# Attention output projection with the four heads packed in 128 rows and channels on partitions

## The chip, the cores and the metric

The kernel runs on one core of a Trainium2 chip. A core has a matrix engine (TensorE, PE in the profile), a vector engine (VectorE, DVE), an activation engine (ScalarE, ACT), a general engine (GpSimd, POOL) and a queue that issues transfers (SyncE, SP). Each takes its own instructions in the order in which the program issues them, and waits at an instruction until what it needs is there. The metric is the time of one execution on the device in microseconds.

## The reference, cut to what matters

Layer 0 is attention with 4 heads of 32 channels over 4 images of 64 x 64 pixels and 128 channels, then a projection, a residual and a norm over the channels. Layer 1 takes its result and adds a 3 x 3 convolution, a spectral term and a mamba block (a selective scan along the pixels). All is float32.

```python
Q, K, V = (split_heads(x_flat @ W + b) for W, b in ((Wq, bq), (Wk, bk), (Wv, bv)))
attn = softmax(einsum('bhnd,bhmd->bhnm', Q, K) * scale)
out = einsum('bhnm,bhmd->bhnd', attn, V)           # then heads side by side: 128 channels
y = out @ Wo + bo + x_flat
y = (y - mean(y)) / sqrt(var(y) + 1e-5) * gamma + beta      # over the 128 channels
# layer 1, per image:
result = conv3x3(y) + irfft2(spec_w @ rfft2(y)) + mamba(y)
# mamba: in_proj, causal conv of 4 taps, silu, dt/B/C, then per pixel
h = exp(dt * A) * h + dt * B * x;  out = sum_n h * C + D * x;  gate with silu(z);  out_proj
```

## The kernel before

**Tiling.** An image's 4096 pixels are 8 chunks of 512, so there are 32 chunks `c`. The heads are taken in two pairs (`PAIRS = 2`), so there are 64 halves `H`: chunk `H // 2`, pair `H % 2`. For each half the keys run in 32 tiles of 128, and one turn of the main loop is one such tile. A chunk is therefore 64 turns, called steps here.

**A loop turn** issues, in this order: the scores of a key tile with their maximum taken off (`scores_for_exp`, six matmuls L478, then the exponential L486 on ACT); the scores for the maximum of the next half, some steps ahead (`scores_for_max`, four matmuls L434, then the maximum L441 on DVE); at an even step one scan of mamba for an earlier chunk (`scan_state`: scan L793 on DVE, then `state` L796, the multiply `hs` L797 and the sum `acc` L812 on GpSimd); at an odd step the next decay (L780 on ACT), the next input term (`db` L785 on GpSimd) and now and then a load of `bc`; then one turn of the planner; then the product of exponentials and values (`times_values`, four matmuls `po` L498). A record in the profile can be half of a float32 matmul, which is why L498 shows four for two calls.

**The planner** orders everything else. A job is a coroutine that yields what it needs next: "P" a slot on TensorE, "D" one on DVE, "A" one on ACT, "B" one of two PSUM banks, "" just the next step. While attention runs an odd step offers two each of P, D and A, an even step only one A. A job that yields "A" and then "PB" thus issues its ACT work in one odd step and its matmuls in the next odd step. The jobs that matter here are `normalise` (divide a pair's output by its softmax sums), `output_projection` (project, add the residual, statistics of the norm, normalise), `mamba_input`, `scan_input` (the convolution steps L673 and L678), `scan_dt` (its last part is three multiplies on GpSimd, L738 to L740), `gate` and `scan_output`.

**Around the projection.** At the end of a half ACT and DVE copy `po` out of PSUM into `oz[k]` (L507, L508), one tile for each pair. In it a head's 32 output rows start at row 0 or 64, with the softmax sum in the row behind them; the other rows are zeros, written once at the start. `normalise` sends the sums to DRAM (`zd`), reads them back spread over the partitions (`zc`), takes the reciprocal, writes it (`rd`), reads it back broadcast over 64 rows for each head (`rz`, L528), and GpSimd multiplies `oz[k]` by it (L531). `output_projection` adds the bias to the residual `xr` on ACT (L546) and then issues, for each of four 128-pixel tiles, one matmul for each pair against a `Wo` padded with zero rows (L554) and one with the identity that adds the residual (L555). The result `py` has pixels on partitions, and DVE takes the statistics from it (L562 to L568) and writes the normalised `xh` (L585).

```python
yield "A"
nc.scalar.activation(xr, xr, AF.Identity, bias=bo)
bank = yield "PB"
```

Of the kernel before, what the change touches and what calls it, by code (L numbers as in the profile page):

```python
# [9 lines left out]
F32 = mybir.dt.float32  # L10
F32R = mybir.dt.float32r
AF = mybir.ActivationFunctionType
ALU = mybir.AluOpType
# [4 lines left out]
P = 128  # L18
W = 64
HEADS = 4  # L20
HD = P // HEADS
PAIRS = HEADS // 2
HS = P // 2
L = 512
RPC = L // W
TPC = L // P
# [129 lines left out]
def attention_then_conv_mamba(  # L156
# [17 lines left out]
    nc = tc.nc  # L174
    ctx.enter_context(tc.manual_schedule())
    B, C, N = x.shape
    NCH = N // L
# [5 lines left out]
    const = ctx.enter_context(tc.tile_pool(name="const", bufs=1))  # L183
    att = ctx.enter_context(tc.tile_pool(name="att", bufs=2))
# [10 lines left out]
    for h in range(HEADS):  # L195
        k, j = divmod(h, 2)
        nc.scalar.dma_start(wk_t[:, h, :], wk[k, :, j * HS : j * HS + HD])
    wat = const.tile([P, 1 + PAIRS, P], F32, name="wat_vo")
    nc.scalar.dma_start(wat[:, 0, :], wvo[0])
    for h in range(HEADS):  # L200
        k, j = divmod(h, 2)
# [3 lines left out]
        )  # L205
    Wk = wk_t.rearrange("c h d -> c (h d)")
    Wv = wat[:, 0, :]
    Wo = [wat[:, 1 + k, :] for k in range(PAIRS)]

    wq_t = const.tile([P, PAIRS, 2, 2, HD], F32, name="wq_t")  # L210
    bq = const.tile([P, PAIRS], F32, name="bq")
# [13 lines left out]
    nc.scalar.dma_start(cst, consts[:, :K_SEL])  # L225
    sel_f = loc.tile([P, P], F32, tag="sg0", name="sel_f", bufs=1)
    nc.scalar.dma_start(sel_f, consts[:, K_SEL:])
    bvk = const.tile([P, PAIRS], F32, name="bvk")
    nc.vector.memset(wat[:, 1:, :], 0.0)
    nc.vector.memset(bvk, 0.0)  # L230
    for h in range(HEADS):
        row = h % 2 * HS
        hs = slice(h * HD, (h + 1) * HD)
        nc.scalar.dma_start(wat[row : row + HD, 1 + h // 2, :], wvo[1, hs, :])
        nc.scalar.dma_start(
            bvk[row : row + HD, h // 2 : h // 2 + 1], bv[0:1, hs].rearrange("o c -> c o")
        )
    vec = const.tile([P, NCOL], F32, name="vec")
    nc.scalar.dma_start(vec, vecs)
    cw = const.tile([P, 9, P], F32, name="cw")  # L240
# [19 lines left out]
    sel = const.tile([P, P], F32R, name="sel")  # L260
    ones = const.tile([P, 1], F32, name="ones")
    nc.vector.memset(ones, 1.0)
    minus_one = const.tile([P, 1], F32, name="minus_one")
    nc.vector.memset(minus_one, -1.0)
    g = const.tile([P, 3, P], F32, name="g")
# [10 lines left out]
    def constants_of_the_rest():  # L276


        yield ""
        half = loc.tile([P, 2, 2 * P], F32, tag="sg1", name="half", bufs=1)  # L280
        nc.vector.tensor_scalar(half, spw, 0.5, None, ALU.mult)
        rr, ir = half[:, 0, :P], half[:, 0, P:]
        ri, ii = half[:, 1, :P], half[:, 1, P:]
        yield ""
        g_id = loc.tile([P, P], F32, tag="ob", name="g_id", bufs=1)
        nc.gpsimd.tensor_tensor(g_id, rr, ii, ALU.add)
        nc.gpsimd.tensor_tensor(cw[:, 4, :], cw[:, 4, :], g_id, ALU.add)
        nc.gpsimd.tensor_tensor(g_flip, rr, ii, ALU.subtract)
        nc.gpsimd.tensor_tensor(g_hil, ri, ir, ALU.subtract)
        nc.gpsimd.tensor_tensor(g_fliphil, ri, ir, ALU.add)  # L290
        yield ""
        nc.vector.tensor_scalar(sbias, cst[:, K_G : K_G + W], col("spec_bi"), None, ALU.mult)
        nc.vector.tensor_tensor(sbias[:, 0:1], sbias[:, 0:1], col("spec_br"), ALU.add)

        nc.scalar.activation(negA, vec[:, COL["A_log"] : COL["A_log"] + NH * NS], AF.Exp)
        yield ""
        nc.vector.tensor_scalar(negA, negA, -1.0, None, ALU.mult)


        bank = yield "PB"  # L300
        pb = bank_tile(bank, [P, 1], "pb")
        for k in range(PAIRS):
            nc.tensor.matmul(pb, Wo[k], bvk[:, k : k + 1], start=k == 0, stop=k == PAIRS - 1)
        yield "D"
        plan.release(bank, 2)
        nc.vector.tensor_tensor(bo, pb, col("bo"), ALU.add)
# [5 lines left out]
        [const.tile([P, L], F32R, name=f"K_{k}_{i}") for i in range(NCH)] for k in range(PAIRS)  # L312
    ]
    VA = [const.tile([P, TPC, HEADS, HD + 1], F32, name=f"V_{i}") for i in range(NCH)]

    oz = [const.tile([P, L], F32, name=f"oz{k}") for k in range(PAIRS)]
    for k in range(PAIRS):
        nc.gpsimd.memset(oz[k], 0.0)
    state = const.tile([P, NH * NS], F32, name="state")
    carry = const.tile([P, NH, TAPS - 1], F32, name="carry")  # L320

# [5 lines left out]
    def bank_tile(bank, shape, name):  # L327
        return psum.tile(shape, F32, tag=f"m{bank}", name=name)
# [136 lines left out]
        nc.vector.scalar_tensor_tensor(mm, mhi, minus_lo, pm, ALU.mult, ALU.subtract)  # L465
        MX[H] = mm

    es, po = {}, {}

    def scores_for_exp(H, m):  # L470

# [17 lines left out]
    def times_values(H, m):  # L489

        k = H % PAIRS
        i, t = divmod(m, TPC)
        assert have["V", i] == H // PAIRS // NCH
        if m == 0:
            po[H] = psum.tile([P, L], F32, tag="o", name=f"po_{H}")
        e = es.pop((H, m))
        for j in range(2):
            nc.tensor.matmul(  # L498
                po[H][used[j], :],
                VA[i][:, t, 2 * k + j, :],  # L500
                e[:, j, :],
                start=m == 0,
                stop=m == NT - 1,
            )
        if m == NT - 1:
            p = po.pop(H)
            nc.scalar.activation(oz[k][used[0], :], p[used[0], :], AF.Identity)  # L507
            nc.vector.tensor_copy(oz[k][used[1], :], p[used[1], :])  # L508

    def normalise(H, t0):  # L510

        k = H % PAIRS
        yield ""
        zd = dram.tile([2, L], F32, tag="zd", name=f"zd_{H}")
        for j in range(2):
            nc.sync.dma_start(zd[j : j + 1, :], oz[k][j * HS + HD : j * HS + HD + 1, :])
        yield ""
        zc = att.tile([P, 2 * L // P], F32, tag="zc", name=f"zc_{H}")
        nc.sync.dma_start(zc, zd.rearrange("h (a c) -> (h a) c", c=2 * L // P))
        yield ""  # L520
        yield ""
        nc.vector.reciprocal(zc, zc)
        rd = dram.tile([2, L], F32, tag="rd", name=f"rd_{H}")
        nc.sync.dma_start(rd.rearrange("h (a c) -> (h a) c", c=2 * L // P), zc)
        yield ""
        r = att.tile([P, L], F32, tag="r", name=f"rz_{H}", bufs=1)
        for j in range(2):
            nc.sync.dma_start(r[rows[j], :], rd[j : j + 1, :].to_broadcast([HS, L]))  # L528
        yield ""
        yield ""  # L530
        nc.gpsimd.tensor_tensor(oz[k], oz[k], r, ALU.mult)  # L531
        if k == PAIRS - 1:
            plan.at(t0, 0, output_projection(H // PAIRS))

    xrs = {}

# [4 lines left out]
    def output_projection(c):  # L541


        xr = xrs.pop(c)
        yield "A"
        nc.scalar.activation(xr, xr, AF.Identity, bias=bo)  # L546
        bank = yield "PB"
        py = bank_tile(bank, [P, TPC, P], f"py_{c}")
        for t in range(TPC):
            if t == TPC // 2:  # L550
                yield "P"
            ts = slice(t * P, (t + 1) * P)
            for k in range(PAIRS):
                nc.tensor.matmul(py[:, t, :], oz[k][:, ts], Wo[k], start=k == 0, stop=False)  # L554
            nc.tensor.matmul(py[:, t, :], xr[:, ts], ident, start=False, stop=True)  # L555


        yield "D"
        st = att.tile([P, TPC, nc.vector.BN_STATS_DIM], F32, tag="st", name=f"st_{c}")
        mv = att.tile([P, TPC, nc.vector.BN_AGGR_DIM], F32, tag="mv", name=f"mv_{c}")  # L560
        for t in range(TPC):
            nc.vector.bn_stats(st[:, t, :], py[:, t, :])  # L562
        for t in range(TPC):
            nc.vector.bn_aggr(mv[:, t, :], st[:, t, :])
        v = att.tile([P, TPC], F32, tag="v", name=f"v_{c}")
        r = att.tile([P, TPC], F32, tag="rs", name=f"r_{c}")
        q = att.tile([P, TPC], F32, tag="q", name=f"q_{c}")
        nc.vector.tensor_scalar(v, mv[:, :, 1], LN_EPS, None, ALU.add)  # L568
        yield ""
        nc.scalar.activation(q, v, AF.Ln)  # L570
        nc.scalar.activation(r, q, AF.Exp, scale=-0.5)
        yield ""
        nc.gpsimd.tensor_tensor(q, r, r, ALU.mult)
        nc.gpsimd.tensor_tensor(q, q, v, ALU.mult)
        nc.gpsimd.tensor_scalar(q, q, -0.5, 1.5, ALU.mult, ALU.add)
        nc.gpsimd.tensor_tensor(r, r, q, ALU.mult)
        yield ""
        yield ""
        yield "D"
        plan.release(bank, 2)  # L580

        xh = loc.tile([P, TPC, P], F32, tag="xh", name=f"xh_{c}", bufs=2)
        XH[c] = xh
        for t in range(TPC):
            nc.vector.tensor_scalar(  # L585
                xh[:, t, :],
                py[:, t, :],
                mv[:, t, 0:1],
                r[:, t : t + 1],
                ALU.subtract,  # L590
                ALU.mult,
            )
# [26 lines left out]
    def mamba_input(c):  # L619
# [7 lines left out]
        nc.gpsimd.memset(xp[:, :, 0 : W + 2 : W + 1], 0.0)  # L627
        if i == 0:
            nc.gpsimd.memset(xp[:, 0, 1 : W + 1], 0.0)
            nc.gpsimd.memset(state, 0.0)  # L630
            nc.gpsimd.memset(carry, 0.0)
        if i == NCH - 1:
            nc.gpsimd.memset(xp[:, RPC + 1, 1 : W + 1], 0.0)
# [153 lines left out]
    def scan_state(c, v):  # L787
# [3 lines left out]
        assert (c, hf) in scaled  # L791
        hs = loc.tile([P, L], F32, tag="hs", name=f"hs_{c}_{k}")
        nc.vector.tensor_tensor_scan(  # L793
            hs, dA.pop((c, v)), db.pop((c, v)), state[:, k : k + 1], ALU.mult, ALU.add
        )
        nc.gpsimd.tensor_copy(state[:, k : k + 1], hs[:, L - 1 :])  # L796
        nc.gpsimd.tensor_tensor(hs, hs, bcs[c, n][:, 1, :], ALU.mult)  # L797
# [302 lines left out]
```

## Time and profile before

| what | value |
|---|---|
| median of 3 runs | 6248.88 us (6247.15 to 6250.07) |
| the profiled execution | 6247.33 us, span 6245.5 us |
| mean granted TensorE clock | 0.978 |
| busy: PE, DVE, ACT, POOL | 96%, 69%, 57%, 74% |
| weight loads on PE | 41% |
| transfers | 404.98 MB, 65 GB/s mean |
| steady part (600 to 4600 us) | PE busy 99% |

A line of the groups gives the source line, engine, operation, what is written from what, the shapes, the count, the busy time and the mean of one in ns, and then the idle time just before the group and what ended it. A line of the timeline gives start and duration in us; a bracket at its end is idle time before it and its releaser. Queues that only issue (ACTq, SPq) have entries of their own. Durations come from the one profiled execution.

### The profile page before, as it was taken

How to read it: one execution, taken by the hardware profiler on the slowest of the kernel's cores; microseconds unless marked ns; L12 is line 12 of the kernel's file. 1: busy time of each engine (PE TensorE's matmuls, PEld its weight loads, DVE VectorE, ACT ScalarE, POOL GpSimd, SP SyncE). 2: the span in 40 equal slices, each digit the busy share in tenths (PEclk: the TensorE clock that was granted, in tenths of full speed). 3: DMA queues.
4: the chain of work that ended last, by engine and by line, in shares of the span. 5: the costliest groups of instructions: out<-in, count | busy, mean ns of one | idle time of the engine just before them, and what ended most of it. 6: DMA issues, size and time to landing. Idle time of an engine off the chain costs nothing.

```text
span 6245.5 us, 83489 instructions
## 1 busy us (share of the span) xinstructions
PE 6001.6 (96%) x32076; PEld 2540.6 (41%) x32076; DVE 4284.2 (69%) x4405; ACT 3582.9 (57%) x4858; POOL 4605.3 (74%) x4951
## 2 busy tenths in 40 slices
PE   5999999999999999999999999999999999999956
PEld 2444444444444444444444444444444444444321
DVE  4556777777777677777767777767776766677556
ACT  1455666665666656566665556656565655665642
POOL 0006887777888777888887788877788877778866
PEclk7999999999999999999999999999999999999976
DMA  3002222223222222223232222222322222212223
GB/s 111 14 15 60 62 58 58 65 65 103 72 75 58 62 62 63 59 65 84 76 87 62 65 62 65 55 60 70 98 70 63 57 52 56 56 53 55 59 68 93
DMA packets 234225, 404.98 MB, mean 65 GB/s; under 512 B 38872, under 2 KB 40416, under 8 KB 233824
## 3 DMA queue, kind: packets, MB, share of 16 engines
q1 hardware_dynamic: 229440, 397.75, 23.3%
q8 instruction: 251, 4.11, 0.3%
q10 hardware_dynamic: 4384, 1.89, 0.1%
q14 instruction: 150, 1.23, 0.1%
HBM read 350.54 MB, written 49.02 MB: 64 GB/s over the span
## 4 chain that ended last, share of the span: by engine, by line
PE 80%; POOL 9%; DVE 5%; ACT 3%; issue 2%; DMA 1%; ACTq 0%; SPq 0%; POOLq 0%; DVEq 0%
PE po L498 27%; PE s L478 25%; PE s L434 13%; PE pf L857 4%; POOL hs L797 3%; DVE part L441 2%; ACT e L486 2%; DVE hs L793 2%; POOL db L785 1%; PE pi L663 1%; PE pdt L713 1%; POOL acc L812 1%; PE pq L410 1%; PE pd L699 1%; PE py L554 1%
## 5 line engine op out<-in xcount | busy, mean ns | idle before, releaser
L441 DVE TENSOR_REDUCE part<-s 128x2 f32<-128x1024 f32 x2048 | 2501.0, 1222 | 1613.6 <-PE s L434 1611.9
L486 ACT ACTIVATE e<-s 128x1024 f32<-128x1024 f32 x2048 | 2094.1, 1023 | 2257.5 <-PE s L478 2249.3
L498 PE MATMUL po<-e,V 128*33 128x512 f32 x8192 | 2160.1, 605 | 2.8 <-DVE oz L508 0.3
L478 PE MATMUL s<-Q,K 64*128 64x512 f32 x8192 | 1500.7, 444 | 25.3 <-ACT e L486 20.2
L793 DVE TENSOR_TENSOR_SCAN hs<-dA,state,db 128x512 f32<-128x512 f32 x1024 | 1305.7, 1275 | 158.9 <-ACT dA L780 69.2
L797 POOL TENSOR_TENSOR hs<-hs,bc 128x512 f32<-128x512 f32 x1024 | 1307.0, 1276 | 82.0
L434 PE MATMUL s<-K,Q 64*128 64x512 f32 x8192 | 1297.7, 395 | 44.4 <-DVE part L441 42.0
L478 PEld LDWEIGHTS s<-Q,K 64*128 64x128 f32 x8192 | 611.5, 185 | 1753.7 <-ACT e L486 1186.1
L785 POOL TENSOR_TENSOR db<-u,bc 128x512 f32<-128x512 f32 x954 | 1223.0, 1282 | 1.6 <-DMA bc<-bcd 1.6
L812 POOL TENSOR_TENSOR acc<-acc,hs 128x512 f32<-128x512 f32 x900 | 1151.7, 1280 | 70.6
L796 POOL COPY state<-hs 128x1 f32<-128x1 f32 x1024 | 212.6, 208 | 976.6 <-DVE hs L793 976.1
L434 PEld LDWEIGHTS s<-K,Q 64*128 64x128 f32 x8192 | 763.7, 186 | 280.5 <-DVE part L441 102.9
L478 PE MATMUL s<-MX,sel 64*128 64x512 f32 x4096 | 810.3, 392 | 0.0
L780 ACT ACTIVATE dA<-dt,negA 128x512 f32<-128x512 f32 x1024 | 702.5, 686 | 146.8 <-DVE hs L793 146.7
L498 PEld LDWEIGHTS po<-e,V 128*33 128x33 f32 x8192 | 299.2, 109 | 899.0 <-issue 865.0
L478 PEld LDWEIGHTS s<-MX,sel 64*128 64x128 f32 x4096 | 383.8, 184 | 90.0
L857 PE MATMUL pf<-xp,cw 128*128 128x512 f32 x576 | 288.2, 617 | 0.0
L450 POOL COPY wide<-mx 128x128 f32<-128x128 f32 x256 | 63.2, 292 | 196.9 <-DVE mx L447 196.9
L806 PE MATMUL acc<-hs,cst 128*128 128x512 f32 x128 | 110.8, 969 | 86.7 <-POOL hs L797 86.7
L531 POOL TENSOR_TENSOR oz<-oz,rz 128x512 f32<-128x512 f32 x64 | 81.9, 1279 | 106.7 <-DMA rz<-rd 106.7
L857 PEld LDWEIGHTS pf<-xp,cw 128*128 128x128 f32 x576 | 96.1, 188 | 131.9 <-issue 126.9
L554 PE MATMUL py<-wat_vo,oz 128*128 128x128 f32 x512 | 83.0, 285 | 22.6 <-POOL oz L531 18.6
(134 smaller groups left out, 3561.0 us busy)
## 6 DMA issues: line engine op xcount, KB each, us to landing
bc<-bcd SPq DMA_DIRECT2D x512, 512.0 KB
K<-kd SPq DMA_DIRECT2D x64, 256.0 KB
rz<-rd SPq DMA_DIRECT2D x128, 128.0 KB
vd<-vst SPq DMA_DIRECT2D x32, 264.0 KB
V<-vd SPq DMA_DIRECT2D x32, 264.0 KB
xq<-in_x SPq DMA_DIRECT2D x32, 256.0 KB
xk<-in_x SPq DMA_DIRECT2D x32, 256.0 KB
kd<-khi SPq DMA_DIRECT2D x32, 256.0 KB
```

The source lines that it names most:

```text
L434: nc.tensor.matmul(sc[:, j, :], QT[H][rows[j], n, t * P : (t + 1) * P], KK[k][m][rows[j], :], start=n == 0, stop=n == 1,)
L441: nc.vector.tensor_reduce(part[H][:, t, :, m], sc, AX.X, ALU.max)
L478: nc.tensor.matmul(s[:, j, :], sel[rows[j], :] if n == 2 else KK[k][i][rows[j], t * P : (t + 1) * P], mov[rows[j], :], start=n == 0, stop= ...
L486: nc.scalar.activation(e, s, AF.Exp)
L498: nc.tensor.matmul(po[H][used[j], :], VA[i][:, t, 2 * k + j, :], e[:, j, :], start=m == 0, stop=m == NT - 1,)
L780: nc.scalar.activation(dA[c, v], dts[c][hf], AF.Exp, scale=negA[:, k : k + 1])
L785: engine.tensor_tensor(db[c, v], us[c][hf], bcs[c, n][:, 0, :], ALU.mult)
L793: nc.vector.tensor_tensor_scan(hs, dA.pop((c, v)), db.pop((c, v)), state[:, k : k + 1], ALU.mult, ALU.add)
L796: nc.gpsimd.tensor_copy(state[:, k : k + 1], hs[:, L - 1 :])
L797: nc.gpsimd.tensor_tensor(hs, hs, bcs[c, n][:, 1, :], ALU.mult)
L812: nc.gpsimd.tensor_tensor(accs[c, hf], accs[c, hf], hs, ALU.add)
L857: nc.tensor.matmul(pf, cw[:, k, :], xps[c][:, dy : dy + RPC, dx : dx + W], start=k == 0, stop=False)
```

## The change

A new tile `op` (the variable `sums`) of 128 rows takes the four heads of a chunk side by side. After each half two transfers copy the heads' 32 output rows from `oz` into their place in it, and the reciprocals are broadcast into the matching 32 rows for each head of one tile `inverse`. GpSimd multiplies once for a chunk, after the second half. The projection is one matmul with `Wo` as the stationary operand and 512 pixels streaming, so that channels lie on partitions; DVE adds the bias and the residual while it takes the result out of PSUM, writing into `xr`; four transposes then bring pixels to the partitions for the norm. `oz` is now one tile from a pool, used by every half in turn. `Wo` is loaded whole, without padding, by one transfer in place of four, and `bv` likewise. The scan of an image's first chunk starts from a tile of zeros; the clearing of `state` is gone.

```diff
-    wat = const.tile([P, 1 + PAIRS, P], F32, name="wat_vo")
+    wat = const.tile([P, 2, P], F32, name="wat_vo")
...
-    bvk = const.tile([P, PAIRS], F32, name="bvk")
-    nc.vector.memset(wat[:, 1:, :], 0.0)
-    nc.vector.memset(bvk, 0.0)
-    for h in range(HEADS):
-        row = h % 2 * HS
-        hs = slice(h * HD, (h + 1) * HD)
-        nc.scalar.dma_start(wat[row : row + HD, 1 + h // 2, :], wvo[1, hs, :])
-        nc.scalar.dma_start(
-            bvk[row : row + HD, h // 2 : h // 2 + 1], bv[0:1, hs].rearrange("o c -> c o")
-        )
+    bvc = const.tile([P, 1], F32, name="bvc")
+    nc.scalar.dma_start(Wo, wvo[1])
+    nc.scalar.dma_start(bvc, bv.rearrange("o c -> c o"))
...
-    oz = [const.tile([P, L], F32, name=f"oz{k}") for k in range(PAIRS)]
-    for k in range(PAIRS):
-        nc.gpsimd.memset(oz[k], 0.0)
...
-            nc.scalar.activation(oz[k][used[0], :], p[used[0], :], AF.Identity)
-            nc.vector.tensor_copy(oz[k][used[1], :], p[used[1], :])
+            oz[H] = att.tile([P, L], F32, tag="oz", name=f"oz_{H}", bufs=1)
+            nc.scalar.activation(oz[H][used[0], :], p[used[0], :], AF.Identity)
+            nc.vector.tensor_copy(oz[H][used[1], :], p[used[1], :])
...
+        c, k = divmod(H, PAIRS)
+        yield ""
+        if k == 0:
+            sums[c] = att.tile([P, L], F32, tag="op", name=f"op_{c}", bufs=1)
+            inverse[c] = att.tile([P, L], F32, tag="r", name=f"rz_{c}", bufs=1)
+        head = [slice((2 * k + j) * HD, (2 * k + j + 1) * HD) for j in range(2)]
+        o = oz.pop(H)
         zd = dram.tile([2, L], F32, tag="zd", name=f"zd_{H}")
         for j in range(2):
-            nc.sync.dma_start(zd[j : j + 1, :], oz[k][j * HS + HD : j * HS + HD + 1, :])
+            nc.sync.dma_start(zd[j : j + 1, :], o[j * HS + HD : j * HS + HD + 1, :])
+        for j in range(2):
+            nc.sync.dma_start(sums[c][head[j], :], o[j * HS : j * HS + HD, :])
...
-        r = att.tile([P, L], F32, tag="r", name=f"rz_{H}", bufs=1)
         for j in range(2):
-            nc.sync.dma_start(r[rows[j], :], rd[j : j + 1, :].to_broadcast([HS, L]))
-        yield ""
-        yield ""
-        nc.gpsimd.tensor_tensor(oz[k], oz[k], r, ALU.mult)
+            nc.sync.dma_start(inverse[c][head[j], :], rd[j : j + 1, :].to_broadcast([HD, L]))
         if k == PAIRS - 1:
-            plan.at(t0, 0, output_projection(H // PAIRS))
+            yield ""
+            yield ""
+            nc.gpsimd.tensor_tensor(sums[c], sums[c], inverse.pop(c), ALU.mult)
+            plan.at(t0, 0, output_projection(c))
...
         xr = xrs.pop(c)
-        yield "A"
-        nc.scalar.activation(xr, xr, AF.Identity, bias=bo)
+        bank = yield "PB"
+        pa = bank_tile(bank, [P, L], f"pa_{c}")
+        nc.tensor.matmul(pa, Wo, sums.pop(c), start=True, stop=True)
+        yield "D"
+        plan.release(bank, 2)
+        nc.vector.scalar_tensor_tensor(xr, pa, bo, xr, ALU.add, ALU.add)
         bank = yield "PB"
         py = bank_tile(bank, [P, TPC, P], f"py_{c}")
         for t in range(TPC):
-            if t == TPC // 2:
-                yield "P"
-            ts = slice(t * P, (t + 1) * P)
-            for k in range(PAIRS):
-                nc.tensor.matmul(py[:, t, :], oz[k][:, ts], Wo[k], start=k == 0, stop=False)
-            nc.tensor.matmul(py[:, t, :], xr[:, ts], ident, start=False, stop=True)
+            nc.tensor.transpose(py[:, t, :], xr[:, t * P : (t + 1) * P], ident)
...
-            nc.gpsimd.memset(state, 0.0)
...
-            hs, dA.pop((c, v)), db.pop((c, v)), state[:, k : k + 1], ALU.mult, ALU.add
+            hs,
+            dA.pop((c, v)),
+            db.pop((c, v)),
+            state[:, k : k + 1] if c % NCH else zero,
```

More of the change, by code (lines that the diff above doesn't have):

```diff
@@ L207, in attention_then_conv_mamba @@
     Wv = wat[:, 0, :]
-    Wo = [wat[:, 1 + k, :] for k in range(PAIRS)]
+    Wo = wat[:, 1, :]
     wq_t = const.tile([P, PAIRS, 2, 2, HD], F32, name="wq_t")
@@ L262, in attention_then_conv_mamba @@
     nc.vector.memset(ones, 1.0)
+    zero = const.tile([P, 1], F32, name="zero")
+    nc.vector.memset(zero, 0.0)
     minus_one = const.tile([P, 1], F32, name="minus_one")
@@ L301, in constants_of_the_rest @@
         pb = bank_tile(bank, [P, 1], "pb")
-        for k in range(PAIRS):
-            nc.tensor.matmul(pb, Wo[k], bvk[:, k : k + 1], start=k == 0, stop=k == PAIRS - 1)
+        nc.tensor.matmul(pb, Wo, bvc, start=True, stop=True)
         yield "D"
@@ L466, in maxima @@
         MX[H] = mm
-    es, po = {}, {}
+    es, po, oz = {}, {}, {}
     def scores_for_exp(H, m):
@@ L506, in times_values @@
             p = po.pop(H)
-            nc.scalar.activation(oz[k][used[0], :], p[used[0], :], AF.Identity)
-            nc.vector.tensor_copy(oz[k][used[1], :], p[used[1], :])
+            oz[H] = att.tile([P, L], F32, tag="oz", name=f"oz_{H}", bufs=1)
+            nc.scalar.activation(oz[H][used[0], :], p[used[0], :], AF.Identity)
+            nc.vector.tensor_copy(oz[H][used[1], :], p[used[1], :])
+    sums, inverse = {}, {}
     def normalise(H, t0):
-        k = H % PAIRS
+        c, k = divmod(H, PAIRS)
         yield ""
+        if k == 0:
[3 more added lines that the diff above has]
+        o = oz.pop(H)
         zd = dram.tile([2, L], F32, tag="zd", name=f"zd_{H}")
         for j in range(2):
-            nc.sync.dma_start(zd[j : j + 1, :], oz[k][j * HS + HD : j * HS + HD + 1, :])
+            nc.sync.dma_start(zd[j : j + 1, :], o[j * HS + HD : j * HS + HD + 1, :])
+        for j in range(2):
+            nc.sync.dma_start(sums[c][head[j], :], o[j * HS : j * HS + HD, :])
         yield ""
@@ L549, in output_projection @@
         for t in range(TPC):
-            if t == TPC // 2:
-                yield "P"
-            ts = slice(t * P, (t + 1) * P)
-            for k in range(PAIRS):
-                nc.tensor.matmul(py[:, t, :], oz[k][:, ts], Wo[k], start=k == 0, stop=False)
-            nc.tensor.matmul(py[:, t, :], xr[:, ts], ident, start=False, stop=True)
+            nc.tensor.transpose(py[:, t, :], xr[:, t * P : (t + 1) * P], ident)
         yield "D"
@@ L793, in scan_state @@
         nc.vector.tensor_tensor_scan(
-            hs, dA.pop((c, v)), db.pop((c, v)), state[:, k : k + 1], ALU.mult, ALU.add
+            hs,
+            dA.pop((c, v)),
+            db.pop((c, v)),
+            state[:, k : k + 1] if c % NCH else zero,
+            ALU.mult,
+            ALU.add,
         )
```

## The prediction

> **What bounds the kernel now.** I read the chain of waits first, then the groups, then the timeline of one chunk (183.1 us in the steady part, 186.6 us in the last sixth).
>
> The chain on the page, share of the span by engine:
> ```profile
> PE 80%; POOL 9%; DVE 5%; ACT 3%; issue 2%; DMA 1%; ACTq 0%; SPq 0%; POOLq 0%; DVEq 0%
> ```
> TensorE sets the time, so what counts is what its in-order queue does and waits for. The groups of the edited lines (columns: busy us, mean ns, idle before, releaser):
> ```profile
> L531 POOL TENSOR_TENSOR oz<-oz,rz 128x512 f32<-128x512 f32 x64 | 81.9, 1279 | 106.7 <-DMA rz<-rd 106.7
> ...
> L554 PE MATMUL py<-wat_vo,oz 128*128 128x128 f32 x512 | 83.0, 285 | 22.6 <-POOL oz L531 18.6
> ```
> The projection hardly ever waits for the GpSimd multiply: 18.6 us in 2 waits, all but 1 us of it in the tail. That looks like slack. The timeline says otherwise. TensorE around one projection (start us, duration us):
> ```profile
> 1211.43 1.05 PE L498 MATMUL po<-e,V 128*33 128x512 f32 x4
> ...
> 1213.76 1.05 PE L498 MATMUL po<-e,V 128*33 128x512 f32 x4
> ...
> 1216.25 0.71 PE L554 MATMUL py<-wat_vo,oz 128*128 128x128 f32 x4
> ...
> 1219.13 1.05 PE L498 MATMUL po<-e,V 128*33 128x512 f32 x4
> ```
> and GpSimd in the same stretch:
> ```profile
> 1206.23 1.30 POOL L738 TENSOR_TENSOR spe<-u,spe 128x512 f32<-128x512 f32 x1
> ...
> 1213.06 1.29 POOL L785 TENSOR_TENSOR db<-u,bc 128x512 f32<-128x512 f32 x1
> 1214.30 1.29 POOL L531 TENSOR_TENSOR oz<-oz,rz 128x512 f32<-128x512 f32 x1
> ```
> The multiply ends at 1214.30 + 1.29 = 1215.59; TensorE takes its result at 1216.25. The margin is 0.66 us. The starts of L531 and L554 over the whole trace give 0.51 to 0.67 us for 26 of the 29 projections c = 2 to 30 and less than nothing for three (two near -0.15, one -1.06). GpSimd is behind there because mamba's three multiplies (L738 to L740) come just ahead. The same lines show the loop's step: 1213.76 - 1211.43 = 2.33 us of matmuls.
>
> **What the Trainium skill says.** "Perfetto Trace Analysis", section Sequencer Loop: an engine instruction sits in its engine's queue until its semaphores are ready. The trace agrees: in the tail TensorE stood 17.9 us at L554 with scan matmuls queued behind. "GPSIMD Engine Reference", section 3.1: a two-input operation takes about 2.6 cycles an element, at 1.2 GHz an estimate of 1.1 us for 512; measured 1.279, which I use. "TensorE: Matmul & The Clock Gate", Part 4: a 128x128 transpose took about 275 ns in a kernel; here each record of L637 is 273 ns, but four follow one another in 0.59 us. "DMA: Bandwidth & Descriptors", Issuing engines are not separate DMA queues: another issuing engine saves only sequencer time; issues on ACT's queue here take 0.38 to 0.44 us.
>
> **The change, part by part.** Steps are counted in a chunk's 64 loop turns.
>
> *TensorE work.* Before, a projection fills 1219.13 - 1216.25 = 2.88 us. After: one f32 128x512 matmul, priced by L663, and four transposes, priced by L637:
> ```profile
> 1643.81 1.13 PE L663 MATMUL pi<-xp,inw 128*128 128x512 f32 x2
> 1644.87 1.05 PE L498 MATMUL po<-e,V 128*33 128x512 f32 x4
> ```
> ```profile
> 1796.17 0.66 PE L637 MATMUL pt<-cst,xh 128*128 128x128 f32 x4
> 1796.76 1.05 PE L498 MATMUL po<-e,V 128*33 128x512 f32 x4
> ```
> That is 1.06 + 0.59, a saving of 1.23 us each, 31 x 1.23 = **-38 us** (the last lies in the tail).
>
> *Where the projection stands.* The old coroutine first yields for an ACT slot (the residual's bias, L546), then for a bank: L546 goes out in step 9, the matmuls in step 11. The new one yields for the bank at once, so in the changed program's instruction order `pa` stands in step 9, ahead of the scores of step 10; the DVE add is in step 11, the transposes in 13. GpSimd's multiply keeps its place, behind the same three multiplies. TensorE reaches `pa` at 1211.43, the operand is ready at 1215.59: **it stands 4.16 us**, and the scores, exponentials and maxima of step 10 stand with it. A hitch of 0.15 us behind L546 goes (1213.76 to 1214.89 is 1.13 where 0.98 is usual). I take 4.1 us for c = 2 to 30: 29 x 4.1 = **+119 us**. Chunks 0 and 1 have no scan yet and margins of 8.6 and 8.5 us: no wait. Bounds: 3.7 (GpSimd's inputs half a microsecond earlier) to 4.8 (as at the three tight ones).
>
> *The other queues' order.* In the last chunks (c = 25 to 30) TensorE already stalls in this stretch:
> ```profile
> 5079.89 0.73 PE L478 MATMUL s<-Q,K 64*128 64x512 f32 x4 [0.91 <-ACT e L486]
> ```
> That and a stall of 0.85 us at 5093 (statistics and a sigmoid step in one turn of DVE) disappear behind the new wait: 6 x 1.8 = **-11 us**. In the steady chunks the norm moves from step 13 to 15, where DVE then has statistics 0.88 + 0.36 + 0.17 to 0.66 and `Q` 0.75 in one turn; the turn leaves it 2.33 - 1.22 = 1.1 us beside the maximum, and the score bank allows 0.56 us of lateness, so about 0.9 us stalls. mamba's convolution steps also double up in steps 33, 35 and 37 (two of 0.75 to 0.81 each): another 1.6 us. Against it go 1.2 us of stalls that now exist (0.64 behind the `oz` copy, which a `pdt` matmul moved to step 1 covers, 0.25 behind `MX`, 0.36 behind `wide`). Net +1.3, taken as +1.0 since 4 us of standing also lets DVE catch up: 21 x 1.0 = **+21 us**, bounds -1.2 and +2.5 each. Chunk c = 2 now has the late pattern and loses it: **-4 us**.
>
> *GpSimd.* One multiply of 1.28 us per chunk goes, that of the first pair, in step 39, where GpSimd waits for DVE anyway (`state` waits 976 us for the scans in all): 0. Memsets of `oz`, `state`: under 2 us, beside waiting: 0.
>
> *ACT and DVE.* 32 passes L546 of 0.713 us go, under TensorE's cover; the add from PSUM comes to DVE at 0.68 to 0.75 us (L609, L416) in step 11, where it fits into the 1.1 us left: 0. It also waits for `pa`; behind it are the next maximum and scan, both already behind `pa` on TensorE.
>
> *SP and the DMAs.* Per pair two more issues (0.4 to 0.5 us each) between `zd` and `zc`, with `xq`, `bc`, `rd` and `rz` behind them. Bytes even out: 128 KB of `op` come, `rz` falls from 256 to 128 KB. Cover: the second `rz` was issued by 1205.15, the multiply began at 1214.30, and none of the steady multiplies waited for it. Without those 9 us every microsecond of lateness would count. The single `oz` buffer is read by DMAs right after it is written and written again 32 steps later: 0. The zero tile: 0.
>
> *Start.* ACT's queue issues eight small loads (14.60 to 18.28) ahead of the first `khi` at 21.85; two remain: 6 x 0.46 = **-3 us**, bounds -3 and 0 if the stores of `vst` bind. *Tail:* the multiply is waited for as now, the norm comes a step or two later: +2, bounds -3 and +6.
>
> Sum: -38 + 119 - 11 + 21 - 4 - 3 + 2 = +86 us. The profiled execution took 6247.33 (span 6245.5), 1.5 below the median 6248.88. 6248.9 + 86 = 6335.
>
> **The rivals.**
> *Faster: the wait does not form.* If GpSimd reached the multiply 4.1 us earlier, the saved matmuls would stay: -38 - 3 - 11 = -52, 6197 us. For it: the page's small wait, and GpSimd idle 26% of the span. Against it: that idle time lies elsewhere in the chunk, and the margin of 0.66 repeats chunk after chunk. It decides at the multiply's end relative to step 9: earlier than TensorE, faster; over 1.3 us later, slower. Chance 0.09.
> *Wait and savings cancel.* The standing lets DVE and GpSimd catch up so well that all stalls of a chunk vanish and the wait is nearer 3 us: 87 - 38 - 11 - 25 - 7 = about +6 to within noise. Chance 0.05.
> *A late transfer.* `op` or `rz` lands after GpSimd gets there, and GpSimd's queue stands too. Five microseconds: 29 x 5 on top, 6480. Against it are the 9 us of cover. Chance 0.03.
> *The likeliest*, `pa` standing behind the multiply: 0.83; its own range is 38 us (stalls at their lower bound) to 118 us (at the upper) above now.
>
> **The numbers.** 6335 is the likeliest case's. The range 6265 to 6370 takes its bounds and part of the cancelling case, leaving out the fast and the late-transfer ones. A measurement here can tell about 0.2% (12 us) from no change: faster 0.09, same 0.05, slower 0.86.
>
> **What would show it.** Right: TensorE waits for GpSimd at `pa` about 29 times for about 4 us, some 119 us where L554 had 18.6; the steady chunk grows from 183.1 to 186 or 188 us; TensorE busy falls by some 38 us; 32 multiplies on GpSimd; `xr` transposes at 0.59 us for four. Wrong: no wait at `pa`, a steady chunk of 182 us or less, or GpSimd waiting for `op` or `rz` in the steady part.

## The result and the profile after

The changed kernel took 6441.63 us (median of 5 runs, 6439.38 to 6445.87) against 6249.77 us for the kernel before on the same chip: 1.031 times as long, 95% interval 1.029 to 1.032. The profiled execution took 6439.82 us (span 6437.3, 191.8 more than before; the mean granted clock fell from 0.978 to 0.964). I had said slower, by 86 us; it is slower by 192.

The chain of waits of the changed kernel, share of the span by engine:

```profile
PE 72%; POOL 15%; DVE 6%; issue 4%; ACT 1%; DMA 1%; ACTq 0%; SPq 0%; POOLq 0%; DVEq 0%
```

TensorE has gone from 80% of the chain to 72%, GpSimd from 9% to 15%. TensorE's waits, by who ended them (us in total, times, longest us), and the group of the new projection:

```profile
PE pa L547 <- POOL op L532: 146.4, 30, 22.5
...
PE s L424 <- DVE part L431: 52.5, 90, 2.9
PE pm L447 <- POOL wide L440: 22.3, 23, 1.0
```

```profile
L547 PE MATMUL pa<-op,wat_vo 128*128 128x512 f32 x64 | 63.3, 1091 | 146.4 <-POOL op L532 146.4
```

The 18.6 us before the old L554 have become 146.4 before `pa`, in 30 waits; one of 22.5 is the tail's. The third row is new: before, `pm` waited for `wide` once, 0.3 us. TensorE's timeline around the projection of one steady chunk (start us, duration us), and GpSimd's last two operations ahead of it:

```profile
1228.30 0.64 PE L424 MATMUL s<-K,Q 64*128 64x512 f32 x4
1233.09 2.08 PE L547 MATMUL pa<-op,wat_vo 128*128 128x512 f32 x2 [4.16 <-POOL op L532]
1235.10 1.92 PE L488 MATMUL po<-e,V 128*33 128x512 f32 x4
1236.95 1.22 PE L468 MATMUL s<-Q,K 64*128 64x512 f32 x4
1237.97 0.63 PE L468 MATMUL s<-MX,sel 64*128 64x512 f32 x2
1238.40 0.74 PE L424 MATMUL s<-K,Q 64*128 64x512 f32 x4
1239.07 1.05 PE L488 MATMUL po<-e,V 128*33 128x512 f32 x4
```

```profile
1230.55 1.27 POOL L783 TENSOR_TENSOR db<-u,bc 128x512 f32<-128x512 f32 x1
1231.78 1.26 POOL L532 TENSOR_TENSOR op<-op,rz 128x512 f32<-128x512 f32 x1
```

The wait is 4.16 us, the figure of the forecast to the last digit. What I had not looked for stands behind it: the same instructions take nearly twice their usual time, `po` 1.92 us where it takes 1.05 a step later. Windows of the same stretch (busy us by engine; the third figure from the end is the granted TensorE clock):

```profile
1229.00:1231.00 2.00, 0.00 (x0) 0.00 (x0) 1.80 (x3) 2.00 (x4) 1.92 (x3) 1.00 0.18 66
1231.00:1233.00 2.00, 0.00 (x0) 0.00 (x0) 0.00 (x0) 0.36 (x1) 2.00 (x3) 0.70 0.60 151
1233.00:1235.00 2.00, 1.91 (x2) 0.50 (x2) 0.00 (x0) 0.00 (x0) 1.84 (x4) 0.50 0.18 50
1235.00:1237.00 2.00, 2.00 (x7) 0.24 (x6) 0.00 (x0) 0.00 (x0) 2.00 (x2) 0.50 0.00 0
1237.00:1239.00 2.00, 2.00 (x12) 1.41 (x10) 0.00 (x0) 0.36 (x1) 1.92 (x3) 0.59 0.00 0
1239.00:1241.00 2.00, 2.00 (x14) 0.96 (x14) 1.82 (x2) 1.19 (x2) 1.92 (x2) 1.00 0.00 0
```

The clock falls to a half some 2.9 us after TensorE's last matmul (0.70 over two us is a fall at 1231.8) and comes back at 1238.6: low for 6.8 us, of which TensorE works 5.5. From one projection to the next the steady chunk takes 191.1 us, 183.1 before; the last ones take 191.0, 186.6 before. TensorE's busy time on the page rose from 6001.6 to 6057.9 us, where the forecast let it fall by 38: slowed matmuls count as busy.

A second difference runs through the whole program. The scores-for-max group, untouched by the change:

```profile
L424 PE MATMUL s<-K,Q 64*128 64x512 f32 x8192 | 1332.7, 403 | 53.2 <-DVE part L431 52.5
```

Before it was 1297.7 us, mean 395 ns. Only part of that is the low clock: in the timeline at clock 1.00 a group mostly reads 0.64 us where it read 0.62.

### The profile page after: what moved, and what is told of

Same layout as the page of the kernel before. It is cut to its first block, busy times and chain, and to the rows that moved or that the text cites. A ratio compares the mean times of both kernels' runs of the same rounds, so it can differ in the third digit from the quotient of the medians.

```text
span 6437.3 us, 82475 instructions
## 1 busy us (share of the span) xinstructions
PE 6057.9 (94%) x31498; PEld 2485.5 (39%) x31498; DVE 4314.9 (67%) x4436; ACT 3573.8 (56%) x4826; POOL 4568.9 (71%) x4913
## 4 chain that ended last, share of the span: by engine, by line
PE 72%; POOL 15%; DVE 6%; issue 4%; ACT 1%; DMA 1%; ACTq 0%; SPq 0%; POOLq 0%; DVEq 0%
PE po L488 24%; PE s L468 22%; PE s L424 12%; POOL hs L800 4%; PE pf L860 4%; POOL db L783 3%; DVE hs L791 3%; DVE part L431 2%; POOL acc L815 2%; PE pdt L711 1%; PE pi L661 1%; PE pq L400 1%; PE pa L547 1%; PE pd L697 1%; POOL state L799 1%
## 5 line engine op out<-in xcount | busy, mean ns | idle before, releaser
L488 PE MATMUL po<-e,V 128*33 128x512 f32 x8192 | 2183.0, 611 | 2.5 <-DVE oz L499 0.3
L424 PE MATMUL s<-K,Q 64*128 64x512 f32 x8192 | 1332.7, 403 | 53.2 <-DVE part L431 52.5
L791 DVE TENSOR_TENSOR_SCAN hs<-dA,state,db 128x512 f32<-128x512 f32 x896 | 1142.5, 1275 | 156.7 <-ACT dA L778 86.4
L424 PEld LDWEIGHTS s<-K,Q 64*128 64x128 f32 x8192 | 762.5, 187 | 305.2 <-DVE part L431 129.8
L547 PE MATMUL pa<-op,wat_vo 128*128 128x512 f32 x64 | 63.3, 1091 | 146.4 <-POOL op L532 146.4
L791 DVE TENSOR_TENSOR_SCAN hs<-dA,zero,db 128x512 f32<-128x512 f32 x128 | 163.1, 1274 | 3.8 <-POOL db L783 3.5
```

What stands on the lines that cost most here:

```text
L424: nc.tensor.matmul(sc[:, j, :], QT[H][rows[j], n, t * P : (t + 1) * P], KK[k][m][rows[j], :], start=n == 0, stop=n == 1,)
L488: nc.tensor.matmul(po[H][used[j], :], VA[i][:, t, 2 * k + j, :], e[:, j, :], start=m == 0, stop=m == NT - 1,)
L791: nc.vector.tensor_tensor_scan(hs, dA.pop((c, v)), db.pop((c, v)), state[:, k : k + 1] if c % NCH else zero, ALU.mult, ALU.add,)
```

## The experiments

The theory: `pa` stands in step 9, where GpSimd's multiply is not done yet; that makes the wait, and the wait makes the low clock. Rival A: the low clock comes from the form of the new matmul. Rival B: what costs is the packing by DMA, the moved schedule or the places of the tiles.

**The projection back in step 11**

```diff
         xr = xrs.pop(c)
+        yield "A"
         bank = yield "PB"
```

> The changed kernel with one more yield for an ACT slot ahead of the bank, so that pa stands in step 11 again (transposes in 15, multiply unmoved). Theory 1 (the place makes the wait, and the wait makes the half clock behind it): no steady wait at pa, no fall of the clock, 29 x (4.16 + 2.5) = 193 us less than the changed kernel, about 6250 us. Rival A (the half clock comes from the new matmul's form, not from the wait): only the wait goes, 29 x 4.16 = 121 us less, about 6320 us. Rival B (the added time is in the packing DMAs, the moved schedule or the longer loop step): 6400 us or more.

Measured: 6204.78 us, 0.9925 of the kernel before (0.991 to 0.994). All of TensorE's waiting at the projection is now the tail's:

```profile
PE pa L548 <- POOL op L532: 22.5, 1, 22.5
```

One yield is worth 237 us, more than the expected 193, since stalls go as well: a steady chunk takes 183.0 us, 8.1 less than in the changed kernel, and one of the last 180.9, 10.1 less. Behind the projections the clock stays at 1.00. Rival B, as the main cause, falls: packing, DVE add and transposes are all still there. Since pa's form is unchanged, so does rival A.

**The kernel before with its projection in step 9**

```diff
         xrs[c] = load_x(c, "xr", 1)
+        for _ in range(5):
+            yield ""
+        yield "A"
+        nc.scalar.activation(xrs[c], xrs[c], AF.Identity, bias=bo)
...
-        yield "A"
-        nc.scalar.activation(xr, xr, AF.Identity, bias=bo)
         bank = yield "PB"
```

> The kernel before, with nothing of the change but the place: the residual's bias is applied in an earlier step, and the projection asks for its bank at once, so that py stands in step 9. Theory 1: py waits 4.1 us for GpSimd's multiply 29 times with the clock at a half behind it, some 29 x 6.6 = 191 us more less about 10 us of late stalls, about 6430 us. Rival B (DMA packing, transposes and norm a step later are what costs): no more than 20 us above the kernel before.

Measured: 6466.31 us, 1.0343 (1.0326 to 1.036). The old form in the new place is as slow as the new form. The wait, and TensorE's work behind it (four `py` matmuls in 1.06 us where before a group of four took 0.71):

```profile
PE py L556 <- POOL oz L531: 132.8, 30, 20.3
```

```profile
1432.18 0.79 PE L556 MATMUL py<-wat_vo,oz 128*128 128x128 f32 x2 [5.54 <-POOL oz L531]
...
1433.19 1.06 PE L556 MATMUL py<-wat_vo,oz 128*128 128x128 f32 x4
```

The place alone makes both the wait and the low clock. It came out 36 us above the expectation; `pm` waits for `wide` 40.5 us here, which I had not counted.

**The same wait, kept warm.** Three further matmuls into the bank of `pa` fill most of the wait and do not shorten it.

```diff
+        for _ in range(3):
+            nc.tensor.matmul(pa, Wo, inw, start=True, stop=True)
         nc.tensor.matmul(pa, Wo, sums.pop(c), start=True, stop=True)
```

> The changed kernel with three further 128x512 f32 matmuls into the bank of pa ahead of pa (their result is overwritten): pa itself starts no earlier, since it still waits for the multiply, but TensorE stands idle about 1 us instead of 4.16. Theory 1 (idling makes the clock fall): clock 1.00 through the stretch, 29 x 2.5 = 72 us less than the changed kernel, about 6370 us. Rival A (form of the matmul or the work behind it): the clock falls as before, about 6442 us.

Measured: 6381.65 us, 1.0209 (1.0194 to 1.0224): 60 us less than the changed kernel, by adding work. Timeline and window:

```profile
1226.52 2.84 PE L548 MATMUL pa<-inw,wat_vo 128*128 128x512 f32 x6
1230.75 1.12 PE L549 MATMUL pa<-op,wat_vo 128*128 128x512 f32 x2 [1.39 <-POOL op L532]
1231.81 1.05 PE L488 MATMUL po<-e,V 128*33 128x512 f32 x4
```

```profile
1231.00:1233.00 2.00, 2.00 (x8) 0.40 (x9) 0.00 (x0) 0.00 (x0) 1.92 (x2) 1.00 0.14 49
```

The scores ahead start at 1225.95, so `pa` comes 4.80 us behind them, 4.79 in the changed kernel (1233.09 - 1228.30); but it runs at clock 1.00, and `po` takes 1.05. The steady chunk is 188.5 us, so the low clock costs 191.1 - 188.5 = 2.6 us there. Behind five of the last six projections it fell nonetheless, here after a standstill of 2.30 us:

```profile
5193.94 1.17 PE L549 MATMUL pa<-op,wat_vo 128*128 128x512 f32 x2 [2.30 <-POOL op L532]
5195.04 1.92 PE L488 MATMUL po<-e,V 128*33 128x512 f32 x4
```

At the sixth, c = 29, TensorE stood 2.28 us and the clock did not fall; the chunk behind it took 189.3 us instead of 190.8.

**A fourth filler**

> The changed kernel with four instead of three further matmuls ahead of pa. With three, TensorE still stood 1.4 us in the steady chunks, where the clock stayed at 1.00, and 2.3 us in the last six, where it fell to a half for about 3.4 us. With a fourth (0.93 us) the standstills are 0.5 and 1.3 us. If a standstill under about 2 us leaves the clock alone: no fall anywhere, and the last six chunks lose 1 to 2 us each: 6 to 12 us less than with three, 6370 to 6376 us, which puts the whole price of the lowered clock at 66 to 72 us. If the late falls had another cause: 6382 us, as with three.

Measured: 6381.41 us, 1.0207 (1.019 to 1.0224). The total missed, the mechanism held. A late chunk:

```profile
5196.85 1.12 PE L549 MATMUL pa<-op,wat_vo 128*128 128x512 f32 x2 [1.42 <-POOL op L532]
5197.91 1.05 PE L488 MATMUL po<-e,V 128*33 128x512 f32 x4
```

No fall behind 1.42 us, and the late chunk goes from 190.9 to 189.3 us. Five fewer falls gain 8 us in the last chunks. Most of that was given back: at the projections of chunks 0 and 1, where no wait covers the filler (`pa` of c = 1 is 2.4 us later than with three), in the chunk that ends at c = 24 (193.0 us, 190.9 with three), where the clock was low for 6.8 us instead of 3.4, and in the tail. The price of the low clock in the changed kernel is thus about 22 x 2.6 + 6 x 1.6 = 67 us.

**A shorter wait**

```diff
         if k == PAIRS - 1:
             yield ""
-            yield ""
             nc.gpsimd.tensor_tensor(sums[c], sums[c], inverse.pop(c), ALU.mult)
```

> The changed kernel with one yield less ahead of GpSimd's multiply, which puts it ahead of one db multiply (1.28 us) on GpSimd; pa stays in step 9. The wait at pa becomes 4.16 - 1.28 = 2.9 us in the steady chunks. In the trace of the changed kernel the clock fell 2.9 to 3.0 us after TensorE's last matmul (idle from 1228.9, clock 0.50 from 1231.9). If the clock falls only behind a longer standstill, it stays at 1.00 here: 29 x (1.28 + 2.5) = 110 us less, about 6332 us. If any wait of a few us lowers it (c = 24 waited 2.27 us, and it fell): only 29 x 1.28 = 37 us less, about 6405 us.

Measured: 6384.48 us, 1.0212 (1.0197 to 1.0227), between the two. The wait is 2.94 us in every steady chunk, but what follows differs. Three chunks in a row, c = 4 to 6:

```profile
1037.38 1.12 PE L546 MATMUL pa<-op,wat_vo 128*128 128x512 f32 x2 [2.94 <-POOL op L531]
...
1225.05 2.08 PE L546 MATMUL pa<-op,wat_vo 128*128 128x512 f32 x2 [2.94 <-POOL op L531]
...
1414.82 1.91 PE L546 MATMUL pa<-op,wat_vo 128*128 128x512 f32 x2 [2.94 <-POOL op L531]
```

Behind the first the clock does not fall at all, behind the second it is low for 6.8 us, behind the third for 3.4, and the chunks that follow take 187.7, 189.8 and 188.9 us. Neither of my two answers was right: the same standstill has three prices.

What decides is where it lies. In the record of the granted clock of each of the 13 traces every low stretch starts on a grid of 3.413 us that runs through the whole execution (to within 0.01 us) and, unless the trace ends in it, lasts a whole number of such windows. The three standstills, cut at that grid (TensorE's busy time is the first figure behind the length):

```profile
1032.73:1036.14 3.41, 1.72 (x12) 0.86 (x10) 3.41 (x4) 2.83 (x5) 3.25 (x5) 1.00 0.04 14
1036.14:1039.56 3.42, 2.18 (x8) 0.58 (x10) 0.17 (x1) 0.73 (x2) 3.34 (x4) 1.00 0.58 144
...
1220.46:1223.88 3.42, 1.65 (x12) 0.86 (x10) 3.42 (x4) 2.84 (x6) 3.26 (x5) 1.00 0.05 19
1223.88:1227.29 3.41, 2.24 (x4) 0.69 (x6) 0.10 (x1) 0.65 (x2) 3.33 (x4) 0.50 0.54 137
...
1411.61:1415.02 3.41, 0.47 (x5) 0.21 (x2) 2.13 (x3) 2.69 (x4) 3.33 (x4) 1.00 0.44 86
1415.02:1418.44 3.42, 3.42 (x6) 0.32 (x5) 0.00 (x0) 0.00 (x0) 3.26 (x4) 0.50 0.54 144
```

The first is split over two windows, each busy for just over half, and nothing happens. The second leaves its first window busy for 1.65 us, just under half: the clock falls at the window's end, and stays low since the next is not full either. The third falls into one window, and one full window later the clock is back. All windows from 600 to 5900 us of the 13 traces bear this out: of those begun at full clock, the clock fell behind all 158 that were busy for less than 48%, behind 6 of 15 between 48 and 55%, and behind none of 2112 between 55 and 99%. Of 17626 at 99% and more it fell behind 12; all held some 2.45 us of the 8-row matmuls `pdt`, and why only some of those lower it stays open. Once low, it stayed low behind all 94 windows under 84% and came back behind all 172 over 88%.

So a standstill of 4.16 us leaves some window less than half busy wherever it lies, and one of 1.4 us alone cannot; in between the place decides. The shortest with a fall behind it was 1.85 us, the longest without one 2.94. In the changed kernel all chunks from c = 4 to 23 take 191.1 us, which is 56 windows, so each of them meets the grid in the same way.

**Places of the tiles: a first try.** The copies of `po` and the packed sums go into the two constant tiles that held `oz`, and `wat_vo` keeps its size.

```diff
-    wat = const.tile([P, 2, P], F32, name="wat_vo")
+    wat = const.tile([P, 1 + PAIRS, P], F32, name="wat_vo")
...
+    ozc = [const.tile([P, L], F32, name=f"oz{k}") for k in range(PAIRS)]
...
-            sums[c] = att.tile([P, L], F32, tag="op", name=f"op_{c}", bufs=1)
+            sums[c] = ozc[1]
```

> The changed kernel with its tiles put where they were before: the copies of po and the packed sums live in the two constant tiles that held oz, wat_vo has its old size, rz is first allocated behind zc. Same instructions. If the longer loop step (2.36 us instead of 2.335) comes from the tiles' places: step 2.335 again, about 64 x 31 x 0.02 = 40 us less, near 6400 us. If not: within 5 us of the changed kernel's 6442 us.

Measured: 6444.48 us, 1.0309 (1.0293 to 1.0324); L424's group is still at 403 ns. That answered a question I had put wrongly. In the compiled program the first tile of K lies 32832 bytes into each partition before, 32352 after the change and 32864 here: a multiple of 64 before, 32 past one in both others. With `Q`, `MX` and `e` it is the other way round: 32 past a multiple before, at one in both others. The tile `zero` takes 32 bytes with its padding.

**K and all behind it moved by 32 bytes, in both directions.** One unused constant ahead of K, in the kernel with `pa` in step 11, in the kernel before, and in the changed kernel; and, in the first of these, a second one behind the state, so that `Q`, `MX` and `e` are at a multiple of 64 too.

```diff
+    pad = const.tile([P, 1], F32, name="pad")
+    nc.vector.memset(pad, 0.0)
     KK = [
```

> The kernel with pa in step 11 and one unused constant of 4 bytes per partition (32 with its padding) ahead of K: K and V begin at a multiple of 64 bytes in a partition again, as in the kernel before, where the change (the tile named zero, the smaller weights) had moved them by 32; Q, MX and e are then at 32 past such a multiple, as before. If the longer scores-for-max group (0.57 us to the next matmul instead of 0.55) comes from K's place: 64 x 0.02 x 31 = 40 us less than with K off the multiple, about 6165 us. If it comes from something else in the new form: about 6205 us, as without.

> The kernel before with nothing changed but that unused constant of 4 bytes (32 with padding) ahead of K, which moves K, V and all behind them by 32 bytes in each partition. If K's place counts: the scores-for-max group goes from 0.55 to 0.57 us, some 40 us more than the kernel before, about 6290 us, since every step of the loop gets longer. If not: within 5 us of 6250.

> The changed kernel with nothing altered but the unused constant ahead of K, which puts K and V at a multiple of 64 bytes again. Theory (places and wait add up): the wait of 4.16 us and the half clock stay, and the scores-for-max group is 0.55 us again: about 22 us less than the changed kernel, 6420 us. Rival (TensorE's time at K is hidden here, since the chunk is held by GpSimd and DVE behind the wait): 6440 us.

> As the one before, with a second such constant behind the state, so that K, V, Q, MX and e all begin at multiples of 64 bytes. If the place of the moving operand of scores-for-exp (Q) also counts, another 64 x 0.02 x 32 = 40 us go, about 6125 us; if only K counts, about 6165 us.

Measured, in this order: 6180.54 us, 0.9887 (0.9873 to 0.9902); 6269.39 us, 1.0031 (1.002 to 1.0043); 6416.49 us, 1.0266 (1.0249 to 1.0283); 6193.22 us, 0.9908 (0.9891 to 0.9924). The group rows of the first two (busy us, mean ns):

```profile
L426 PE MATMUL s<-K,Q 64*128 64x512 f32 x8192 | 1298.5, 395 | 40.5 <-DVE part L433 40.2
```

```profile
L436 PE MATMUL s<-K,Q 64*128 64x512 f32 x8192 | 1322.2, 400 | 42.1 <-DVE part L443 40.6
```

Moved by 32 bytes, the kernel before loses 19 us and its group grows from 1297.7 to 1322.2; put back, the other two gain 24 and 25. The sign is as expected three times. The size is about half of the expected 40 in the first two, since 0.55 and 0.57 are rounded and the difference is nearer 0.012 us (24.5 us over 2048 groups); in the third it is 25 for 22, and there the low stretches of the clock change too (6.8, 6.8 and 3.4 us in turn instead of 6.8 each). But these three move `Q`, `MX` and `e` the other way at the same time. The fourth run parts the two, against both of its answers: with only K, V and the state moved, the kernel with `pa` in step 11 goes from 6204.78 to 6193.22 us, and moving `Q`, `MX` and `e` off the multiple as well gives the other 13. Each accounts for about half; which operand it is, and how, these runs do not settle.

**The other cure: the multiply two steps earlier**

```diff
         if k == PAIRS - 1:
-            yield ""
-            yield ""
             nc.gpsimd.tensor_tensor(sums[c], sums[c], inverse.pop(c), ALU.mult)
```

> The changed kernel with K at a multiple of 64 bytes, pa left in step 9, and GpSimd's multiply issued two steps earlier, which puts it ahead of mamba's three multiplies (some 8 us earlier on GpSimd). If the wait comes from pa's place against the multiply's, it goes, and the clock stays at 1.00: 124 + 67 + 22 us less than the changed kernel, about 6225 us or, with the late stalls gone as in the kernels with pa in step 11, down to 6180 us. Rival (a late transfer): rz is issued until 9 us ahead of the old place of the multiply, so here GpSimd waits for rz, mamba's multiplies and the scan's inputs come later, and TensorE waits again: 6280 us or more.

Measured: 6264.68 us, 1.0024 (1.0016 to 1.0032), between the two answers. TensorE's waits:

```profile
PE s L426 <- DVE part L433: 71.0, 115, 2.9
PE pa L547 <- POOL op L532: 25.6, 6, 21.4
PE pm L449 <- POOL wide L442: 25.5, 23, 2.3
```

The wait at `pa` is gone but for the tail and five short ones, and the mean clock is 0.978 again; a late transfer can be only a small part of the rest (GpSimd waited for `rz` 29.5 us once at the start, as in the changed kernel, and 18.6 us in twelve short waits). Yet it is 84 us slower than the kernel with `pa` in step 11 and K in the same place. TensorE waits for the maxima 71.0 us, 40.2 there, which is 31 of them. Part of that is the norm's place, which is the changed kernel's (55.4 us there with K moved back). That the remainder comes from mamba's multiplies, which now follow 1.27 us later, is not shown.

The fastest version is the one with `pa` in step 11 and K at a multiple of 64: 6180.54 us, 1.1% under the kernel before.

## Why the prediction was right and wrong, point by point

**The wait: right.** 22 waits of 4.16 us, one of 2.27 (c = 24, where I had 4.1), six of 5.03 to 5.04: 124 us for +119. The step in which `pa` stands, read from the order of the instructions, and the end of GpSimd's multiply gave it.

**The clock: the step that failed.** "It stands 4.16 us, and the scores, exponentials and maxima of step 10 stand with it" was priced as 4.1 us and no more. TensorE's work behind a standstill was taken at the durations of a busy stretch. Measured: another 2.6 us in a steady and 1.6 in a late chunk, **+67 us**, more than half of the miss of 106. The trace of the kernel before showed it once: behind a wait of 2.75 us for `acc` the same `po` took 1.92 us instead of 1.05.

```profile
4733.87 3.78 PE L914 MATMUL py<-acc,outw 128*128 128x512 f32 x4 [2.75 <-POOL acc L904]
4737.58 1.92 PE L498 MATMUL po<-e,V 128*33 128x512 f32 x4
```

The Trainium skill has it too, and the prediction did not use it: "TensorE: Matmul & The Clock Gate", section What's actually happening, says that the clock halves behind an idle window of about 3.4 us, counted on a window that runs freely and does not start with the kernel. The grid of 3.413 us and the low stretches of one or two windows agree; that the whole window has to be idle does not, since here one busy for less than 48% was enough. Its section Why this matters for your kernels asks for no gaps over about 3 us; in these runs 1.85 us were enough where they fell into one window.

**The tiles' places: a term that was missing.** "The zero tile: 0" is wrong, not for its work but for the 32 bytes by which it moves K and all behind it: 19 to 25 us by the three comparisons.

**TensorE's work: right.** In the version with `pa` in step 11 the projection takes 1.06 us and the transposes 0.59, so the -38 stands.

**The stalls: late right, steady undersized.** These are remainders, not measured one by one. A late chunk grew by 4.4 us: 5.03 + 1.6 + 0.75 (64 groups of 0.012) - 1.23 leaves -1.75 for its stalls, where I had -1.8. A steady one grew by 8.0: 4.16 + 2.6 + 0.75 - 1.23 leaves +1.7, where I had +1.0. The turn with the statistics and `Q` is as foretold; VectorE, then TensorE in the changed kernel:

```profile
1253.57 0.88 DVE L561 BATCH_NORM_STATS2 st<-py 128x6 f32<-128x128 f32 x4
1254.37 0.36 DVE L563 BATCH_NORM_AGGREGATE mv<-st 128x2 f32<-128x6 f32 x4
1254.76 0.71 DVE L567 TENSOR_SCALAR v<-mv 128x4 f32<-128x4 f32 x1
1255.39 0.74 DVE L406 SCALAR_TENSOR_TENSOR Q<-pq,bq,Q 128x512 fp32r<-128x512 f32 x1
```

```profile
1257.31 0.74 PE L424 MATMUL s<-K,Q 64*128 64x512 f32 x4 [0.69 <-DVE part L431]
...
1288.32 1.02 PE L447 MATMUL pm<-cst,wide 128*128 128x128 f32 x4 [1.00 <-POOL wide L440]
```

The second line is what I had the wrong way round: I let 0.36 us behind `wide` go, and got 1.00. The 1.6 us for the convolution steps were about 0.6 in one steady chunk.

**The sum.** -38 + 124 + 67 + 24 - 11 + 36 (21 x 1.7) - 4 - 3 + 2 = 197, for 191.8 between the spans; the 36 and the -11 are the remainders above, so the sum closes in part by construction. The forecast's lower end, 38 above, is 40 by its own terms, which changes nothing. My 86 lacked the clock and the 32 bytes, 91 us together.

**The rivals.** The faster one was sound as a mechanism and wrong about its trigger: GpSimd's multiply ahead of step 9 takes the wait away, but gave 6264.68 us, K moved back included, instead of 6197. `pa` behind the multiply gives the gain, and more than the -52, because the late chunks fall to 180.5 us. Wait and savings did not cancel: the wait stayed at 4.16 us, and a steady chunk's stalls grew. A late transfer held up nothing in the steady part of the changed kernel.

## What to carry to other kernels

Before a wait of a few microseconds is put on the engine that sets the time, price it twice: what it stands, and what it does more slowly afterwards; the granted clock by windows shows the second part, and it depends on how the wait lies against the clock's own windows. A step that is asked for earlier is not sooner done: look at where its operand's last producer stands in its own queue, and move the consumer behind it rather than the producer ahead of its neighbours. When an untouched group of instructions has grown a little everywhere, look at where its tiles lie.

## What was not expected of the hardware

- Filling a standstill with matmuls whose result is thrown away made the program 60 us faster, since TensorE's clock fell to 0.50 behind every standstill of 4.16 us and behind none of 1.39.
- A standstill of 2.94 us cost nothing in one chunk, 6.8 us of low clock in the next and 3.4 in the one after. The clock fell at the edges of a fixed grid of 3.413 us, behind all 158 windows that TensorE was busy for less than 48% and none of the 2112 between 55 and 99%.
- K, V and the state, moved by 32 bytes within a partition, were worth 12 us, and `Q`, `MX` and `e`, moved by 32 bytes, another 13; with both the four 64x512 matmuls took some 12 ns longer together, 24.5 us in 2048 groups. How the places act stays open.
